# Rows of one tile in every 22nd pair fetched singly by SyncE, and states cleared tile by tile

## The chip, the cores and the metric

The kernel runs on one core of one Trainium2 chip. The metric is the device time of one launch in microseconds (us), as the median of several runs.

## What is computed

The reference is one layer of a graph network (GATv2 with pre-normalization) over 12500 nodes of 128 features and 400000 edges, with a residual and a feed-forward block. The edges come sorted by destination. Cut to what matters here:

```python
h = jnp.maximum(_layernorm(x), 0.0)
x_l = (_ln(h) @ W_l).reshape(n, H, C)          # H = 8 heads, C = 16
x_r = (_ln(h) @ W_r).reshape(n, H, C)
e = (ea @ W_e).reshape(-1, H, C)
m = jax.nn.leaky_relu(x_l[src] + x_r[dst] + e, 0.2)
alpha = jnp.einsum('ehc,hc->eh', m, att)
# softmax of alpha over the edges of each destination, then
out = segment_sum(x_l[src] * a[:, :, None], dst)
h = h + out + bias
return x + h + gelu(_ln(h) @ W1 + b1) @ W2 + b2
```

The costly part is `x_l[src]`: for each of the 400000 edges (and padding) a row of x_l is fetched from DRAM by its source index.

## The kernel before, in words

Nodes lie in 98 tiles of 128. A **preamble** normalizes x, computes x_l for all nodes and writes it to DRAM (`xl_dram`, rows of 136 floats: 128 features and 8 ones, 544 bytes). Its order is written out by hand in rounds `r` (line 784 onwards): at r = 14 the source indices are loaded (`src_sb`, line 797), `as_float` (line 439) and `x_l` (line 595, with its store at 603) run on VectorE (DVE) in their rounds. For 29 chosen pairs of the main loop ("raw" or late pairs) the preamble instead gathers rows of x itself on GpSimd (POOL), and their x_l rows are made later; these pairs need no gather in the main loop.

The **main loop** (`window_edges`) handles 782 pairs. A pair is two units of 256 sorted edges: 512 edges, four tiles of 128 edges. The loop is a software pipeline written out by hand: in round r each stage handles pair r minus its lateness. The stages that matter:

- `gather` (line 972), four rounds ahead: four indirect DMAs on POOL's queue, one per tile, each fetching 128 rows of `xl_dram` into `xs` (line 980). For a late pair, one plain DMA from `late_dram` on SyncE's (SP's) queue instead (line 975). `xs` has twelve buffers.
- `windows` (line 988), three rounds ahead, in every fourth round: four DMAs on SP's queue (`ea`, `dl`, `du`, `zw`, lines 994 to 1010); the address of `zw` comes from a register that SP loads from the SBUF (line 955).
- `place` on DVE (line 1020) turns `dl` into indicator columns in `ea`.
- `combine` on TensorE (PE): four transposes of `xs` (line 1034) and a matmul with `ea` (line 1037) into `z`; then slope, max, scores, minimum, exponent, transposes (lines 1043 to 1088).
- `collect` (line 1097), six rounds late: PE multiplies the turned weights with `xs`.
- `own_heads` (lines 1106 and 1112), seven rounds late, on DVE: the records `rec` of the pair.
- `put` (line 1122), seven rounds late, on SP's queue, last in the round: the records go to the tensor `state` in DRAM, at an address from a register (four addresses are loaded in every fourth round). Records of neighbouring pairs may touch the same nodes, so each store waits for the landing of the one before.

`state` must hold neutral values before the stores come: `clear(g)` (line 743) writes the constant `empty` over seven tiles of nodes, one DMA for each of two states. Group 0 is cleared at the end of the preamble; the other 13 in every eighth round, in the middle of the round.

Until about round 196 SP also loads `ea_s` in every second round for a mean over the edge features (line 1129). Finished groups of four node tiles load their states (`f_state`, line 1173) and go through the feed-forward block in later rounds.

SP issues its DMAs in the order of the program. The program gives them eight semaphores in turn, so that each DMA waits for the landing of the eighth before it. Gathers on POOL have eight semaphores of their own.

Of the kernel before, what the change touches and what calls it, by code (L numbers as in the profile page):

```python
# [13 lines left out]
F32 = mybir.dt.float32  # L14
BF16 = mybir.dt.bfloat16
I32 = mybir.dt.int32
U8 = mybir.dt.uint8
# [5 lines left out]
P = 128  # L23
# [19 lines left out]
OW = 172  # L43
OS = 176
PW = OR * OS
BEFORE = 12
AFTER = 3
WN = P - DE
# [14 lines left out]
BUSY = 5  # L63
LEAD = 2
KEPT = 7
BIG = 2.0**126
CAP = 2.0**120

# [59 lines left out]
def raw_pairs(nt, n_edges):  # L128

    n_pr = -(-n_edges // (UP * U))  # L130
    at = [xr_round(t, nt, n_edges) + XR_STEPS + 1 for t in range(GN, nt, GN)]
    at = at[:-1] + [r + RAW_SHIFT for r in at[:RAW_MORE]]
    return [(r + RAW_STEPS + AHEAD + 1, r) for r in at if r + RAW_STEPS + AHEAD + 2 < n_pr]


def heads_of(nc, pool, out, att_c, fh):
# [8 lines left out]
def tile_gnn(  # L145
# [56 lines left out]
    src_sb = keep.tile([P, NCH * K], I32, name="src_sb")  # L202
    base_sb = keep.tile([1, NU // UP], I32, name="base_sb")
    win_sb = keep.tile([1, NU // QU], I32, name="win_sb")
    flag = keep.tile([1, 1], I32, name="flag")
    quads = [(t, min(GN, NT - t)) for t in range(0, NT, GN)]
    VAR = 6
# [532 lines left out]

    empty = keep.tile([P, H, SH], F32, name="empty")

    def clear(g):
        for st in state:
            nc.sync.dma_start(
                st.rearrange("(t p h) f -> p t (h f)", p=P, h=H)[:, g * GT : (g + 1) * GT, :],
                empty.rearrange("p h f -> p (h f)")[:, None, :].to_broadcast([P, GT, SW]),
            )

    node_stages = (  # L750
        (0, x_stats),
# [16 lines left out]
    with tc.manual_schedule():  # L768
        load_first()
        make_identity(nc, ident)  # L770
        for t in xls:
            nc.vector.memset(t[:, :, P:], 1.0)
        load_weights()
        load_x(0, min(GN, NT))
        load_raw()
        load_x(GN, min(3 * GN, NT - GN))
        for t in range(4 * GN, NT, 14):
            load_x(t, min(14, NT - t))
        load_dst()
        load_consts()  # L780
        nc.vector.memset(empty, 0.0)
        nc.vector.memset(empty[:, :, C + 1 : SH], CAP)
        rows_at = [i * 5 // 4 for i in range(len(raw))]
        for r in range(max(max(len(qs), 9) + LAST + 1, 16 + PARTS, rows_at[-1] + KEPT + 1)):
            if r == 0:
                count_up()
            for d, at in zip(raw, rows_at):
                if r == at:
                    raw_gather(d)
                if r == at + KEPT:  # L790
                    raw_store(d)
            if r == 3:
                weights()
            if r == 9:
                last_of_units()
            if r == 14:
                nc.sync.dma_start(src_sb, src)
# [24 lines left out]
        clear(0)  # L822
    pre.close()

    fast = nc.values_load(flag[0:1, 0:1], min_val=0, max_val=1)
    with tc.If(fast == 1) as cmp:
        window_edges(
            tc, n_edges, ea_t, NT, NE, NUE, ident, wer, weh, negrep, diag, nid, farw, bias_r, b2_r, w1_sb, w2_sb,
            cols, xl_dram, xl_t, xr_dram, xr_t, dc_dram, du_dram, late_dram, state_dram, state, clear, xr_steps, qs, raw_steps, raw, x_t, out_t, h_sb, src_sb, base_sb, win_sb, wid,
        )  # L830
    with cmp.Else():
        any_edges(
# [64 lines left out]

def window_edges(
    tc, n_edges, ea_t, NT, NE, NUE, ident, wer, weh, negrep, diag, nid, farw, bias_r, b2_r, w1_sb, w2_sb,
    cols, xl_dram, xl_t, xr_dram, xr_t, dc_dram, du_dram, late_dram, state_dram, state, clear, xr_steps, qs, raw_steps, raw, x_t, out_t, h_sb, src_sb, base_sb, win_sb, wid,  # L900
):


# [25 lines left out]
    with ExitStack() as es:  # L929
# [34 lines left out]
        def states_at(at):  # L964
# [4 lines left out]
                "u (n f) -> n u f", f=SH * 4  # L969
            )  # L970

        def gather(c):
            xs = rows.tile([P, KP, XW], F32, name="xs")
            if c in of_raw:
                nc.sync.dma_start(xs, late_dram[of_raw[c]["i"]])
                pairs[c]["xs"] = xs
                return
            for t in tiles_of(c):
                for j in t:
                    nc.gpsimd.indirect_dma_start(  # L980
                        out=xs[:, j, :],
                        out_offset=None,
                        in_=xl_dram,
                        in_offset=bass.IndirectOffsetOnAxis(ap=src_sb[:, c * KP + j : c * KP + j + 1], axis=0),
                    )
            pairs[c]["xs"] = xs
# [42 lines left out]
        def combine(c):  # L1029

            d, e = pairs[c], sum(edges_of(c))
            z = ps2.tile([P, EPR], F32, name="z")
            for j in range(e // P):
                nc.tensor.matmul(  # L1034
                    z[:, j * P : (j + 1) * P], d["xs"][:, j, 0:P], ident, start=(j == 0), stop=False, is_transpose=True
                )
            nc.tensor.matmul(z[:, :e], d["zw"], d["ea"][:, :e], start=False, stop=True)  # L1037
            d["z"] = z
# [51 lines left out]
        def collect(c):  # L1090
# [4 lines left out]
            for i, js in enumerate(tiles_of(c)):  # L1095
                for j in js:
                    nc.tensor.matmul(  # L1097
                        d["acc"][:, i, :], d["pt"][:, j * P : (j + 1) * P], d["xs"][:, j, :],
                        start=(j == js[0]), stop=(j == js[-1]),
                    )  # L1100

# [836 lines left out]
```

## Time and profile before

| | |
|---|---|
| median of 3 runs | 3961.41 us (3957.83 to 3962.45) |
| the profiled execution's own time | 3956.45 us |
| its span, first to last instruction | 3954.7 us |
| mean granted TensorE clock | 0.943 |
| DMA moved over the span | 552.09 MB, mean 140 GB/s |

The profile shows one execution. Busy time counts an engine's work, not its waits; for SP the rows named SPq are its issuing of DMAs, its register loads and its moves, in three numbers the least, the median and the longest in ns. In a row of waits stand the total in us, how often, and the longest. In a timeline row stand the start in us, the duration in us, engine, line and operation; in brackets the idle time before it. "issue" is time in which an engine waited for nothing that the profile shows.

### The profile page before, as it was taken

The numbers are of one execution on the slowest core, as the hardware profiler recorded it, in microseconds if no ns is written. First come the engines' busy times: TensorE is split into PE (matmuls) and PEld (weight loads), VectorE is DVE, ScalarE is ACT, GpSimd is POOL, SyncE is SP. The second block draws the span as 40 slices with busy tenths as digits, with TensorE's granted clock in tenths as the row PEclk, the third lists the DMA queues.
The fourth block names the chain that finished last, engine by engine and source line by source line (L and its number), as shares of the span: only waits on it lengthen the run. The fifth ranks groups of instructions, "written<-read, shape, count | busy, mean of one in ns | idle before, by whom it ended". The sixth has DMA issues, their size and how long they took to land. (4 is left out here: it accounts for less than half of the span.)

```text
span 3954.7 us, 58500 instructions
## 1 busy us (share of the span) xinstructions
PE 3447.8 (87%) x18462; PEld 2358.8 (60%) x18463; DVE 2792.9 (71%) x6137; ACT 2168.7 (55%) x4747; POOL 2956.0 (75%) x3138
## 2 busy tenths in 40 slices
PE   4589898989898899999898898998889899889898
PEld 3356565656565666666665665666666566556565
DVE  6577777878776767677767776777767667667665
ACT  7445555655565555555555555555555555455444
POOL 7777777777777777777777777777777777777774
PEclk6799999999999999999999999999999999999999
DMA  8777787777666666666566666556556665655553
GB/s 225 214 183 190 195 201 194 184 176 168 164 128 124 128 122 123 128 123 120 115 122 128 124 123 128 123 119 125 117 124 125 127 122 108 122 119 114 122 118 74
DMA packets 579318, 552.09 MB, mean 140 GB/s; under 512 B 286689, under 2 KB 457282, under 8 KB 578578
## 3 DMA queue, kind: packets, MB, share of 16 engines
q1 hardware_dynamic: 478280, 330.80, 35.9%
q0 software_dynamic: 100000, 217.32, 28.5%
q8 instruction: 150, 2.46, 0.3%
q14 instruction: 168, 1.38, 0.1%
q10 hardware_dynamic: 720, 0.13, 0.0%
HBM read 482.05 MB, written 65.88 MB: 139 GB/s over the span
## 5 line engine op out<-in xcount | busy, mean ns | idle before, releaser
L980 POOL DMA_INDIRECT xs<-xl_dram,src_sb x3009 | 2841.7, 944 | 917.1 <-issue 798.0
L1075 ACT ACTIVATE p<-ab,rec 128x256 f32<-128x256 f32 x1563 | 655.2, 471 | 1025.8 <-DVE rec L1064 1021.3
L1106 DVE TENSOR_TENSOR own<-acc,diag 128x272 f32<-128x272 f32 x782 | 341.4, 437 | 811.5 <-PE acc L1097 809.5
L1097 PE MATMUL acc<-xs,pt 128*128 128x136 f32 x6250 | 891.6, 288 | 0.3 <-DVE own L1106 0.3
L1034 PE MATMUL z<-ident,xs 128*128 128x128 f32 x3125 | 552.9, 283 | 374.0 <-DMA xs<-xl_dram,src_sb 324.9
L1037 PE MATMUL z<-ea,zw 128*128 128x512 f32 x1564 | 852.7, 628 | 26.5 <-DVE ea L1020 11.3
L1034 PEld LDWEIGHTS z<-ident,xs 128*128 128x128 f32 x3125 | 398.4, 143 | 768.4 <-DMA xs<-xl_dram,src_sb 413.6
L1097 PEld LDWEIGHTS acc<-xs,pt 128*128 128x128 f32 x6250 | 820.7, 199 | 0.5 <-DVE own L1106 0.5
L1058 PE MATMUL ab<-m,negrep 128*128 128x512 f32 x1564 | 806.4, 597 | 0.0
L1088 ACT COPY pt<-pt_ps 128x512 f32<-128x512 f32 x782 | 454.9, 582 | 570.9 <-PE pt_ps L1083 568.9
L1053 DVE TENSOR_TENSOR m<-z,zs 128x512 f32<-128x512 f32 x782 | 532.8, 681 | 139.2 <-ACT zs L1048 138.1
L1083 PEld LDWEIGHTS pt_ps<-ident,p 128*128 128x128 f32 x3125 | 415.9, 148 | 360.1 <-issue 286.4
L1020 DVE TENSOR_SCALAR ea<-dl,wid 96x516 f32<-96x516 bf16 x782 | 575.8, 736 | 36.1 <-DMA dl<-dc_dram 36.1
L1064 DVE TENSOR_REDUCE rec<-ab 128x2 f32<-128x512 f32 x781 | 538.0, 689 | 13.1 <-PE ab L1058 12.5
L1083 PE MATMUL pt_ps<-ident,p 128*128 128x128 f32 x3125 | 499.4, 285 | 1.2 <-ACT xr L627 0.9
L1048 ACT ACTIVATE zs<-z 128x512 f32<-128x512 f32 x782 | 472.7, 604 | 41.7 <-DMA xs<-xl_dram,src_sb 34.9
L1112 DVE TENSOR_REDUCE rec<-own 128x34 f32<-128x272 f32 x782 | 340.8, 436 | 26.7
L1043 PE MATMUL ab<-ne,farw 128*128 128x512 bf16 x782 | 313.0, 400 | 28.4 <-ACT p L1075 25.7
L1037 PEld LDWEIGHTS z<-ea,zw 128*128 128x128 f32 x1564 | 256.5, 205 | 30.1 <-DVE ne L1027 10.3
L1058 PEld LDWEIGHTS ab<-m,negrep 128*128 128x128 f32 x1564 | 245.1, 194 | 1.1 <-DMA ea_s<-in_ea_t 0.7
L1043 PEld LDWEIGHTS <-farw 128*128 128x128 bf16 x782 | 79.5, 102 | 221.9 <-issue 110.2
L1075 ACT ACT_TABLE_LOAD x104 | 133.4, 1283 | 1.8
(237 smaller groups left out, 2167.4 us busy)
## 6 DMA issues: line engine op xcount, KB each, us to landing
dl<-dc_dram SPq DMA_DIRECT2D x196, 396.0 KB
ea<-in_ea_t SPq DMA_DIRECT2D x196, 256.0 KB
ea_s<-in_ea_t SPq DMA_DIRECT2D x98, 512.0 KB
xs<-xl_dram,src_sb POOLq DMA_INDIRECT x3009
state<-empty SPq DMA_DIRECT2D x28, 504.0 KB
state<-rec SPq DMA_DIRECT2D x781, 18.0 KB
f_st<-state SPq DMA_DIRECT2D x46, 288.0 KB
du<-du_dram SPq DMA_DIRECT2D x196, 64.0 KB
```

Source lines behind the costliest of these rows:

```text
L980: nc.gpsimd.indirect_dma_start(out=xs[:, j, :], out_offset=None, in_=xl_dram, in_offset=bass.IndirectOffsetOnAxis(ap=src_sb[:, c * KP + j ...
L1020: nc.vector.tensor_scalar(d["ea"][0:WN].rearrange("p (a b) -> p a b", b=OW), d["dl"][0:WN].rearrange("p (a b) -> p a b", b=OS)[:, :, 0:OW] ...
L1034: nc.tensor.matmul(z[:, j * P : (j + 1) * P], d["xs"][:, j, 0:P], ident, start=(j == 0), stop=False, is_transpose=True)
L1037: nc.tensor.matmul(z[:, :e], d["zw"], d["ea"][:, :e], start=False, stop=True)
L1048: nc.scalar.activation(d["zs"][:, :e], d["z"][:, :e], AF.Copy, scale=SLOPE)
L1053: nc.vector.tensor_tensor(d["m"][:, :e], d["z"][:, :e], d["zs"][:, :e], op=OP.max)
L1058: nc.tensor.matmul(d["ab"][:, :e], negrep.rearrange("p n h -> p (n h)"), d["m"][:, :e], start=False, stop=True)
L1064: nc.vector.tensor_reduce(d["rec"][:, :, CX], d["ab"].rearrange("p (u e) -> p u e", e=U), AX.X, OP.min)
L1075: nc.scalar.activation(d["p"][:, us], d["ab"][:, us], AF.Exp, bias=d["rec"][:, i, CX:SH], scale=-1.0)
L1083: nc.tensor.transpose(d["pt_ps"][:, js], d["p"][:, js], ident)
L1088: nc.scalar.copy(d["pt"][:, :e], d["pt_ps"][:, :e])
L1097: nc.tensor.matmul(d["acc"][:, i, :], d["pt"][:, j * P : (j + 1) * P], d["xs"][:, j, :], start=(j == js[0]), stop=(j == js[-1]),)
```

## The change

Two things change.

First, in 35 pairs (31, 53, 75 and so on, every 22nd) the fourth tile isn't gathered by POOL. SP fetches its 128 rows one by one, each with a DMA of 544 bytes at an address from a register, into one of two new tiles `hand0` and `hand1`. The 128 DMAs are spread over 22 rounds, five or six at the start of each round, and end three rounds before `combine` uses the tile. The addresses come from a table `hand_sb` of source indices times the row's size, loaded in the preamble at r = 14 and multiplied on DVE at r = 16; SP loads 26 of them into registers at a time. `combine` and `collect` read the new tile through `row_of`.

Second, `clear` handles one tile of nodes for both states in one DMA. Four tiles are cleared at the end of the preamble, the other 94 one in every fourth round, at the very end of the round, behind `put`.

```diff
+CLEARED = 4
+CLEAR = 4
+HAND_EVERY = 22
+HAND_FIRST = 31
+HAND_LEAD = 2
+HAND_READ = 26
+def hand_pairs(nt, n_edges):
+    late = {c for c, _ in raw_pairs(nt, n_edges)}
+    hands = range(HAND_FIRST, n_edges // (UP * U), HAND_EVERY)
+    assert not late & set(hands)
+    return hands
...
-    def clear(g):
-        for st in state:
-            nc.sync.dma_start(
-                st.rearrange("(t p h) f -> p t (h f)", p=P, h=H)[:, g * GT : (g + 1) * GT, :],
-                empty.rearrange("p h f -> p (h f)")[:, None, :].to_broadcast([P, GT, SW]),
-            )
+    def clear(t):
+        both = state_dram[0 : UP * SR].rearrange("(a n) f -> a n f", a=UP)
+        nc.sync.dma_start(
+            both[:, (BEFORE + t * P) * H : (BEFORE + (t + 1) * P) * H].rearrange("a (p h) f -> p a (h f)", h=H),
+            empty.rearrange("p h f -> p (h f)")[:, None, :].to_broadcast([P, UP, SW]),
+        )
...
             if r == 14:
                 nc.sync.dma_start(src_sb, src)
+                nc.sync.dma_start(
+                    hand_sb,
+                    bass.AP(
+                        tensor=src.tensor, offset=src.offset + (hands[0] + 1) * UP * KU - 1,
+                        ap=[[hands.step * UP * KU, len(hands)], [NCH * K, P]],
+                    ),
+                )
+            if r == 16:
+                nc.vector.tensor_scalar(hand_sb, hand_sb, float(XW * 4), None, op0=OP.mult)
...
-        clear(0)
+        for t in range(CLEARED):
+            clear(t)
...
+        def hand(r):
+            i, k = divmod(r + HAND_LEAD + hands.step - hands[0], hands.step)
+            if not 0 <= i < len(hands):
+                return
+            d = by_hand[hands[i]]
+            if k == 0:
+                d["x"] = once.tile([P, XW], F32, name=f"hand{i % 2}")
+            for e in range(P * k // hands.step, P * (k + 1) // hands.step):
+                if e % HAND_READ == 0:
+                    d["at"] = words(hand_sb[i : i + 1, e : min(e + HAND_READ, P)], (NT * P - 1) * XW * 4)
+                nc.sync.dma_start(
+                    d["x"][e : e + 1, :].bitcast(U8), rows_at(xl_dram, d["at"][e % HAND_READ], 1, XW * 4)
+                )
+        def row_of(c, j):
+            return by_hand[c]["x"] if c in by_hand and j == KP - 1 else pairs[c]["xs"][:, j, :]
...
                 for j in t:
+                    if c in by_hand and j == KP - 1:
+                        continue
                     nc.gpsimd.indirect_dma_start(
...
-        CLEAR = 8
         with tc.manual_schedule():
             for r in range(-AHEAD, max(last_round, groups[-1]["round"] + 18)):
                 in_round(r, early, groups[:-2])
+                hand(r)
...
-                if r > 0 and r % CLEAR == 0 and r // CLEAR < NT // GT:
-                    clear(r // CLEAR)
...
                 for late, f in late_stages:
                     c = r - late
                     if 0 <= c < n_pr:
                         f(c)
+                t, off = divmod(r, CLEAR)
+                if off == 0 and CLEARED <= t + CLEARED < NT and t >= 0:
+                    clear(t + CLEARED)
```

More of the change, by code (lines that the diff above doesn't have):

```diff
@@ L204, in tile_gnn @@
     win_sb = keep.tile([1, NU // QU], I32, name="win_sb")
+    hands = hand_pairs(NT, n_edges)
+    hand_sb = keep.tile([len(hands), P], I32, name="hand_sb")
     flag = keep.tile([1, 1], I32, name="flag")
@@ L828, in tile_gnn @@
             tc, n_edges, ea_t, NT, NE, NUE, ident, wer, weh, negrep, diag, nid, farw, bias_r, b2_r, w1_sb, w2_sb,
-            cols, xl_dram, xl_t, xr_dram, xr_t, dc_dram, du_dram, late_dram, state_dram, state, clear, xr_steps, qs, raw_steps, raw, x_t, out_t, h_sb, src_sb, base_sb, win_sb, wid,
+            cols, xl_dram, xl_t, xr_dram, xr_t, dc_dram, du_dram, late_dram, state_dram, state, clear, xr_steps, qs, raw_steps, raw, x_t, out_t, h_sb, src_sb, base_sb, win_sb, hand_sb, hands, wid,
         )
@@ L899, in window_edges @@
     tc, n_edges, ea_t, NT, NE, NUE, ident, wer, weh, negrep, diag, nid, farw, bias_r, b2_r, w1_sb, w2_sb,
-    cols, xl_dram, xl_t, xr_dram, xr_t, dc_dram, du_dram, late_dram, state_dram, state, clear, xr_steps, qs, raw_steps, raw, x_t, out_t, h_sb, src_sb, base_sb, win_sb, wid,
+    cols, xl_dram, xl_t, xr_dram, xr_t, dc_dram, du_dram, late_dram, state_dram, state, clear, xr_steps, qs, raw_steps, raw, x_t, out_t, h_sb, src_sb, base_sb, win_sb, hand_sb, hands, wid,
 ):
@@ L970, in states_at @@
             )
+        by_hand = {c: {"i": i} for i, c in enumerate(hands)}
+        def hand(r):
[13 more added lines that the diff above has]
+            return by_hand[c]["x"] if c in by_hand and j == KP - 1 else pairs[c]["xs"][:, j, :]
         def gather(c):
@@ L1034, in combine @@
                 nc.tensor.matmul(
-                    z[:, j * P : (j + 1) * P], d["xs"][:, j, 0:P], ident, start=(j == 0), stop=False, is_transpose=True
+                    z[:, j * P : (j + 1) * P], row_of(c, j)[:, 0:P], ident, start=(j == 0), stop=False, is_transpose=True
                 )
@@ L1097, in collect @@
                     nc.tensor.matmul(
-                        d["acc"][:, i, :], d["pt"][:, j * P : (j + 1) * P], d["xs"][:, j, :],
+                        d["acc"][:, i, :], d["pt"][:, j * P : (j + 1) * P], row_of(c, j),
                         start=(j == js[0]), stop=(j == js[-1]),
```

## The prediction

> **What bounds the kernel now.** I read the busy shares first, then the group of the gathers, then the first and the last gather in the timeline, then who waits for them.
>
> ```profile
> PE 3447.8 (87%) x18462; PEld 2358.8 (60%) x18463; DVE 2792.9 (71%) x6137; ACT 2168.7 (55%) x4747; POOL 2956.0 (75%) x3138
> ```
> ```profile
> L980 POOL DMA_INDIRECT xs<-xl_dram,src_sb x3009 | 2841.7, 944 | 917.1 <-issue 798.0
> ```
> ```profile
> 151.60 0.94 POOL L980 DMA_INDIRECT xs<-xl_dram,src_sb  x1 [0.30 <-issue]
> ...
> 3909.17 0.94 POOL L980 DMA_INDIRECT xs<-xl_dram,src_sb  x1 [0.31 <-issue]
> ```
> ```profile
> PE z L1034 <- DMA xs<-xl_dram,src_sb: 324.9, 247, 4.1
> ```
>
> By share PE looks like the bound and POOL looks a quarter idle. The group says otherwise: 2841.7 us busy and 917.1 us idle make 3758.8 us for 3009 gathers, and 0.30 us of "issue" stands ahead of each. From 151.60 to 3909.17 lie 3008 steps of 1.249 us: POOL hardly ever waits for anybody between the first gather and the last. PE meanwhile waits 324.9 us for gathers to land. So POOL's issuing of gathers sets the length of the loop, at 1.249 us each, and each gather taken away is worth that much until something else is late.
>
> **What the change takes away.** 35 pairs (31, 53, ... 779) gather three tiles instead of four: 35 x 1.249 = 43.7 us off the engine that sets the end. No gather is replaced on POOL. PE is the next engine; it must give up 43.7 of its 324.9 us of waiting, so it doesn't become the bound. Its transposes and its collecting matmuls read the new tile instead of xs, same shapes, plus some seven semaphore waits for each such pair, hidden in the same waiting.
>
> **What it adds.** 35 x 128 = 4480 one-row DMAs on SP's queue (about 5.8 in each round, ahead of the round's other work), 175 register loads of up to 26 words, one small table load and one DVE multiply in the preamble, and 98 clears of one tile and both states in place of 28 of seven tiles and one state. All hang on SyncE, so its queue has to be priced. These are its rows: a stretch of it, its operations, its one-row DMAs, its waits, and the landing of stores in the chain that ended last.
>
> ```profile
> 1011.56 0.41 SPq L994 DMA_DIRECT2D ea<-in_ea_t  x1
> 1012.03 0.42 SPq L999 DMA_DIRECT2D dl<-dc_dram  x1
> 1012.50 0.60 SPq L1004 DMA_DIRECT2D du<-du_dram  x1
> 1014.00 0.34 SPq L1010 DMA_DIRECT2D zw<-xr_dram  x1
> 1016.20 0.41 SPq L1122 DMA_DIRECT2D state<-rec  x1
> 1016.66 0.47 SPq L1129 DMA_DIRECT2D ea_s<-in_ea_t  x1
> ```
> ```profile
> L1122 SPq MOVE state<-rec x782: 29/29/38, 183.0 to 3930.3; - x196
> L1122 SPq DMA_DIRECT2D state<-rec x782: 350/395/1278, 192.0 to 3930.4; - x196
> ```
> ```profile
> L955 SPq TENSOR_LOAD <-win_sb x196: 527/748/812, 158.7 to 3896.8; - x196
> L955 SPq TENSOR_LOAD <-base_sb x196: 299/307/331, 182.6 to 3926.9; - x196
> ```
> ```profile
> L745 SPq DMA_DIRECT2D state<-empty x28: 377/488/687, 153.4 to 665.0; - x28
> ```
> ```profile
> L1010 SPq DMA_DIRECT2D zw<-xr_dram x196: 332/343/359, 159.6 to 3897.6; - x196
> ```
> ```profile
> 27.89 0.22 SPq L328 DMA_DIRECT2D dc<-in_dst  x1
> 28.16 0.32 SPq L333 DMA_DIRECT2D dc<-in_dst  x1
> 28.52 0.27 SPq L337 DMA_DIRECT2D dc<-in_dst  x1
> ```
> ```profile
> SPq L1122 <- DMA state<-rec: 1359.2, 547, 8.2
> SPq L1122 <- DVE rec L1112: 739.1, 425, 8.9
> SPq L1122 <- DMA state<-empty: 85.8, 14, 9.3
> ```
> ```profile
> 3926.48 1.65 DMA state<-rec
> ...
> 3928.27 2.02 DMA state<-rec
> ```
>
> SP's work repeats every four rounds. Today: one set of windows, 2.83 us (1011.56 to 1014.34 and the gap behind); four stores at about 0.52 with move, semaphore and gaps, 2.1; one load of four bases, 0.36. While the edge sums are loaded (two rounds of every four, until about round 196) 1.04 more. The late rows and x_r add about 0.25, the finishing groups later about 0.35. That is 6.6 us early and 5.9 us after round 196. The rest of SP's time is waiting, 1359.2 us for a store's landing and 739.1 us for DVE. This waiting is the cover for the new DMAs: they stand between a store and the next one.
>
> Available for four rounds at the new pace: 16 gathers less those that late pairs (29 with no gather, 11 of them in the first 196 rounds) and the new pairs save. Early (784 - 44 - 8) / 196 x 4 x 1.249 = 18.7 us; later about 19.1 us.
>
> Price of a one-row DMA: no row shows one with an address from a register. Bounds: 0.22 us, the shorter of two rows of one descriptor (L328; the other, L337, took 0.27), and 0.395, the store's median, with a register address and 256 pieces. zw, with a register address and 96 rows, takes 0.343; L333, 96 rows and a fixed address, 0.32, so the register costs about 0.02. I take 0.25, between the two one-row rows, plus 0.03 for the move and two gaps of 0.045: 0.37 each. Four rounds hold 23.3 of them, 8.6 us. Register loads: 0.9 per four rounds at 0.75 plus gap, 0.7 us (0.3 by the other row).
>
> The clears: every fourth round until about round 376 one DMA of 0.49 plus gap stands right behind a store of the same tensor and waits for its landing, 1.65 to 2.02 us by the chain: 2.5 us per four rounds. Behind that wait stand the next round's one-row DMAs, its windows and its store. The next store waits for the clear's landing, which the one-row DMAs between them cover. The 85.8 us of waits for the big clears go, but nothing late hung on them, so that is worth nothing.
>
> Sum for SP in four rounds: early 6.6 + 8.6 + 0.7 + 2.5 = 18.4 of 18.7 us; rounds 196 to 376 17.7 of 19.1; then 15.2 of 19.2. It fits, early by a hair. Windows are fetched three rounds ahead, records of stores have eleven buffers, and the one-row tiles are complete three rounds before their use, so SP may lag some 10 us before anyone else waits. I charge 2 us for stretches where a landing is slow.
>
> **Preamble.**
>
> ```profile
> 71.97 0.70 SPq L797 DMA_DIRECT2D src_sb<-in_src  x1
> ...
> 136.65 0.37 SPq L603 DMA_DIRECT2D xl_dram<-xl  x1
> ```
> ```profile
> 43.91 0.61 SPq L266 DMA_DIRECT2D first_sb<-in_dst  x1
> ```
> ```profile
> 77.81 0.42 DVE L439 CAST df<-dc 98x512 f32<-98x512 int32 x1
> ```
>
> The table of 4480 single words is issued right behind src_sb at 72.7; 784 single words took 0.61 us to issue, so 0.6 to 3.5 us here. DVE multiplies it just ahead of the cast that ran at 77.81, so DVE waits for the landing, behind the whole of src_sb. What DVE loses moves the last x_l store from 136.65; the first gather at 151.60 needs that landed (2 us), so 13 us of cover. Bounds: 0 us lost, and some 10 us if DVE stands for more than 20. I take 2.
>
> **Sum.** -43.7 + 2 + 2 = -39.7 us. The profiled execution took 3956.45 us (span 3954.7), giving 3916.7; the median of the runs is 4.96 higher, 3961.41, so **3922**.
>
> [...]
>
> **Rivals.**
> 1. SP becomes the bound in the early loop. For: SP fits with 0.3 us to spare, and landings are slower there. Against: the one-row rows. If each costs 0.34 like zw (0.46 with move and gaps, 10.7 us per four rounds), SP needs 20.5 of 18.7 early and 19.8 of 19.1 until round 376: 49 x 1.8 + 45 x 0.7 = 120 us lost, less 10 of lag: 3922 + 110 = 4032, slower. It cancels the gain at about 0.30 us an issue (19.6 of 18.7, 49 x 0.9 = 44): that price decides.
> 2. The same with the store's price, 0.395 (12.0 us per four rounds): 49 x 3.1 + 45 x 2.0 = 242, so about 4164. The rows of one descriptor speak against it. [...]
> 3. The preamble's wait exceeds its cover: 3922 + 10 = 3932, still faster.
> 4. It doesn't do what it says: the program still issues all gathers. The code skips them, so I leave it out.
>
> **Chances.** Forecast, with small overruns, 0.55; rival 1 in its degrees 0.27; rival 2 0.08; rival 3 0.07; anything else 0.03. Range: the floor is all 43.7 us and 8 us of noise and luck at the ends, 3910; the top is rival 1 at zw's price, 4032, rounded to 4035. Rival 2 and a little more stay out. Faster by over 0.2% (8 us, about what a measurement of this kernel can tell from no change): the forecast, rival 3 and no more, less small overruns, 0.58; within 0.2%, rival 1 near its break-even, 0.08; slower 0.34. The likeliest case alone would be 3912 to 3940.
>
> **What would show it.** Right: 2974 gathers at 1.249 us without gaps, the last one starting near 3867; SP's one-row DMAs at 0.22 to 0.28 us; SP's waits at the store for DVE smaller but still there. Wrong: gaps between POOL's gathers in the first 1900 us, ended by PE; DVE waiting for dl (L1020) or PE for the one-row tile; stores lagging their records by over 10 us; DVE idle for long at the new multiply.

## The result, and the profile after

The changed kernel takes **4393.13 us** (median of 4 runs, 4387.0 to 4399.74) beside 3960.08 us for the kernel before in the same comparison: a ratio of 1.1094, 95% interval 1.1075 to 1.1113. The change costs 433 us where a gain of 39 was forecast, and the time lies far above the top of the range. The profiled execution has a span of 4385.2 us at a mean granted clock of 0.902 (before: 3954.7 us at 0.943).

Line numbers of the changed kernel are some 50 higher than before: the gathers are L1029, the one-row DMAs L1011, all register loads L981, the clears L761, the stores of the states L1171, the window mask L1069. The first lines are the busy shares and the group of the gathers.

```profile
PE 3542.8 (81%) x18462; PEld 2425.4 (55%) x18463; DVE 2794.4 (64%) x6138; ACT 2146.4 (49%) x4747; POOL 2923.4 (67%) x3103
```
```profile
L1029 POOL DMA_INDIRECT xs<-xl_dram,src_sb x2974 | 2808.9, 945 | 1357.7 <-issue 777.1 <-PE acc L1146 496.1 <-DMA xs<-xl_dram,src_sb 33.8
```

The 35 gathers are gone and a gather still costs 0.945 us, so the gain was booked as forecast. But POOL now stands idle 1357.7 us, and 496.1 of these end with a collecting matmul of PE: a buffer for the gathered rows comes free too late. POOL is no longer the bound. PE is busy 95.0 us longer than before for the same 18462 instructions, with the lower clock; how much of the 433 us that adds was not tested. Who is late first is in the waits of all engines (waited for; us in total, times, longest):

```profile
DVE ea L1069 <- DMA dl<-dc_dram: 598.3, 134, 11.3
POOL xs L1029 <- PE acc L1146: 496.1, 159, 12.7
PE z L1086 <- DMA zw<-xr_dram: 265.4, 57, 9.7
```

DVE waits for a window row (dl), PE for another (zw), up to 11 us at a time. Both are fetched by SyncE, three rounds ahead. So SyncE is behind, and its own waits say that it has no air left:

```profile
SPq L761 <- DMA state<-rec: 251.6, 91, 4.8
SPq L1171 <- DMA state<-rec: 120.8, 184, 3.3
SPq L1011 <- DMA dl<-dc_dram: 105.1, 136, 2.1
...
SPq L1171 <- DVE rec L1161: 35.1, 78, 3.9
```

The last row is the one to read. When SyncE waits at a store for DVE's record, it is ahead of the computation. It did so for 739.1 us before and does so for 35.1 us now. What it waits for instead are landings: 251.6 us at the clears, for the store just ahead of them. The one-row DMAs (L1011) wait too, 105.1 us for dl: each DMA waits for the landing of the eighth before it, and that can be one of the windows.

The rows of SyncE's new operations (duration in ns: minimum, median, maximum):

```profile
L1011 SPq DMA_DIRECT2D hand<-xl_dram x4480: 224/228/397, 187.7 to 4325.1; - x195
```
```profile
L981 SPq TENSOR_LOAD <-win_sb x196: 556/805/870, 159.6 to 4327.5; - x196
L981 SPq TENSOR_LOAD <-base_sb x196: 302/562/765, 189.3 to 4353.6; - x196
L981 SPq TENSOR_LOAD <-hand_sb x175: 1619/2132/5929, 185.7 to 4308.6; - x175
```

A one-row DMA takes 0.228 us, inside the forecast 0.22 to 0.28. A register load of 26 words was forecast at 0.75 us and takes 1.6 to 5.9. Summed over its 175 records that is 602 us, 3.44 each, in two heaps: the first, third and fifth load of a tile take 2.16, 1.92 and 1.74 us on average, the second and the fourth 5.68 and 5.70. In SyncE's timeline (start us, us from the first to the last of a stretch of like instructions) such a load is hidden inside a stretch of one-row DMAs:

```profile
1310.48 0.42 SPq L1171 DMA_DIRECT2D state<-rec  x1
1310.99 1.90 SPq L1011 DMA_DIRECT2D hand<-xl_dram  x6
1314.21 0.42 SPq L1171 DMA_DIRECT2D state<-rec  x1
1314.75 7.33 SPq L1011 DMA_DIRECT2D hand<-xl_dram  x4
```

Six DMAs in 1.90 us are 0.32 a step; the four below took 7.33 because a load of 5.58 us stands among them. Both kinds are on the chain of work that ended last, the loads (L981) with 4% of the span and the one-row DMAs (L1011) with 4%:

```profile
PE 38%; DMA 24%; DVE 12%; SPq 11%; issue 5%; ACT 5%; POOL 2%; DVEq 0%; ACTq 0%; POOLq 0%
PE acc L1146 9%; PE z L1086 9%; PE ab L1107 7%; DMA dl<-dc_dram 7%; DMA state<-rec 6%; PE pt_ps L1132 5%; SPq L981 4%; SPq L1011 4%; PE z L1083 3%; DMA zw<-xr_dram 3%; DMA du<-du_dram 3%; PE ab L1092 2%; DVE ea L1069 2%; DVE rec L1113 2%; POOL xs L1029 2%
```

Where the loss falls is seen from the gathers in two stretches (POOL's busy time and its instructions):

```profile
300.00:1000.00 700.00, 417.92 (x443) 0.86 0.61 142
2000.00:3500.00 1500.00, 1054.89 (x1118) 0.93 0.57 117
```

The kernel before has 561 and 1201 gathers there. The first stretch lost 21%, the second 7%. By the starts of the stores, the change lags the kernel before by 245 us at pair 196, by 373 us at pair 376 and by 427 us at the last pair: most is lost early.

### The profile page after: what moved, and what is told of

Same layout as the page of the kernel before. It is cut to its first block, busy times and chain, and to the rows that moved or that the text cites. A ratio compares the mean times of both kernels' runs of the same rounds, so it can differ in the third digit from the quotient of the medians.

```text
span 4385.2 us, 67585 instructions
## 1 busy us (share of the span) xinstructions
PE 3542.8 (81%) x18462; PEld 2425.4 (55%) x18463; DVE 2794.4 (64%) x6138; ACT 2146.4 (49%) x4747; POOL 2923.4 (67%) x3103
## 4 chain that ended last, share of the span: by engine, by line
PE 38%; DMA 24%; DVE 12%; SPq 11%; issue 5%; ACT 5%; POOL 2%; DVEq 0%; ACTq 0%; POOLq 0%
PE acc L1146 9%; PE z L1086 9%; PE ab L1107 7%; DMA dl<-dc_dram 7%; DMA state<-rec 6%; PE pt_ps L1132 5%; SPq L981 4%; SPq L1011 4%; PE z L1083 3%; DMA zw<-xr_dram 3%; DMA du<-du_dram 3%; PE ab L1092 2%; DVE ea L1069 2%; DVE rec L1113 2%; POOL xs L1029 2%
## 5 line engine op out<-in xcount | busy, mean ns | idle before, releaser
L1029 POOL DMA_INDIRECT xs<-xl_dram,src_sb x2974 | 2808.9, 945 | 1357.7 <-issue 777.1
L1086 PE MATMUL z<-ea,zw 128*128 128x512 f32 x1564 | 903.8, 662 | 437.7 <-DMA zw<-xr_dram 265.4
L1069 DVE TENSOR_SCALAR ea<-dl,wid 96x516 f32<-96x516 bf16 x782 | 576.9, 738 | 606.6 <-DMA dl<-dc_dram 598.3
L1146 PE MATMUL acc<-xs,pt 128*128 128x136 f32 x6180 | 907.0, 293 | 21.5 <-DVE own L1155 12.2
L1146 PEld LDWEIGHTS acc<-xs,pt 128*128 128x128 f32 x6180 | 835.9, 204 | 24.4 <-DVE own L1155 12.9
L1107 PE MATMUL ab<-m,negrep 128*128 128x512 f32 x1564 | 816.9, 605 | 0.0
L1083 PEld LDWEIGHTS z<-ident,xs 128*128 128x128 f32 x3090 | 387.4, 145 | 535.0 <-issue 303.2
L1132 PEld LDWEIGHTS pt_ps<-ident,p 128*128 128x128 f32 x3125 | 427.8, 152 | 404.8 <-issue 309.0
L1083 PE MATMUL z<-ident,xs 128*128 128x128 f32 x3090 | 489.7, 280 | 189.6 <-issue 84.1
L1132 PE MATMUL pt_ps<-ident,p 128*128 128x128 f32 x3125 | 516.0, 292 | 20.9 <-ACT pt L1137 15.4
L1184 DVE TENSOR_REDUCE part<-ea_s 128x1 f32<-128x1024 f32 x98 | 119.0, 1214 | 104.1 <-DMA ea_s<-in_ea_t 103.9
```

Of the source, the lines that this page charges most:

```text
L1029: nc.gpsimd.indirect_dma_start(out=xs[:, j, :], out_offset=None, in_=xl_dram, in_offset=bass.IndirectOffsetOnAxis(ap=src_sb[:, c * KP + j ...
L1069: nc.vector.tensor_scalar(d["ea"][0:WN].rearrange("p (a b) -> p a b", b=OW), d["dl"][0:WN].rearrange("p (a b) -> p a b", b=OS)[:, :, 0:OW] ...
L1083: nc.tensor.matmul(z[:, j * P : (j + 1) * P], row_of(c, j)[:, 0:P], ident, start=(j == 0), stop=False, is_transpose=True)
L1107: nc.tensor.matmul(d["ab"][:, :e], negrep.rearrange("p n h -> p (n h)"), d["m"][:, :e], start=False, stop=True)
L1132: nc.tensor.transpose(d["pt_ps"][:, js], d["p"][:, js], ident)
L1146: nc.tensor.matmul(d["acc"][:, i, :], d["pt"][:, j * P : (j + 1) * P], row_of(c, j), start=(j == js[0]), stop=(j == js[-1]),)
```

## The experiments

Two groups of chips have to be kept apart. On one the kernel before took 3961 us, as in the first comparison. On four others it took 4716 to 4765 us, and its trace shows other gaps there (last section). Every run below is given by its ratio to the kernel before on its own chip, with that kernel's time.

**The theories at the start.** A: SyncE is full over the whole loop; its register loads are the largest part of the excess, the clears' wait for the store ahead of them the second. B: the 4480 one-row DMAs alone fill it. C: the clears alone do it.

**The change once more**, unaltered, as a measure for its neighbours:

> The change itself once more, as the measure for its neighbours: the four runs before this one stood against a kernel before of 4716 us in place of 3960, so times go by their ratio to it. 1.109 if this chip behaves as the first one; any other ratio shows what the chip does to the change, and the neighbours are compared with this one.

Measured 5162.53 us beside 4722.09, ratio 1.0931 (1.0907 to 1.0954): 440 us lost on this chip too.

**Clears as before.**

```
-                t, off = divmod(r, CLEAR)
-                if off == 0 and CLEARED <= t + CLEARED < NT and t >= 0:
-                    clear(t + CLEARED)
+                if r > 0 and r % CLEAR == 0 and r // CLEAR < NT // GT:
+                    clear(r // CLEAR)     # CLEAR = 8, seven tiles, ahead of the round's stores
```

> The change, but with the clears as they were: 28 of seven tiles, one state each, in every eighth round, in the middle of the round. Theory A (SyncE is full over the whole loop; its register loads of 26 words, 3.5 us on average where 0.75 was forecast, are the largest part of the excess, the clears' wait for the store ahead of them, 251.6 us by the profile of the change, the second): about 240 us of waiting go over the first 376 rounds and some 40 come with the big clears, so about 4190. Rival B (the 4480 one-row DMAs alone fill SyncE, the wait at a clear only takes the place of waits elsewhere): within 40 us of the change's 4393. Rival C (the clears alone are what made the change slow): about 3925.

Measured 5114.63 beside 4715.9, ratio 1.0844 (1.0813 to 1.0875). Some 40 us by the difference of the ratios, not 200: C falls here. For A's second term the run says little, because the clears wait much less on such a chip. In the traces of two further runs on this chip with the new clears, below, SyncE waits 67.3 us there (one load) and 78.1 us (loads put first), 34 times each, against 251.6 (91 times) on the first chip.

**One register load for all one-row DMAs.**

```
-                if e % HAND_READ == 0:
-                    d["at"] = words(hand_sb[i : i + 1, e : min(e + HAND_READ, P)], ...)
+                if not fixed:
+                    fixed.extend(words(hand_sb[0:1, 0:8], ...))
```

> The change with a single register load of eight words ahead of the first one-row DMA instead of 175 of up to 26 words: all 4480 one-row DMAs are issued as before, but from eight addresses over and over, so the rows of the new tiles are not those of the reference. Theory A: SyncE gives up 175 x 3.47 = 607 us of work; in rounds up to 376 all of the 0.79 us of each round is gained, later only some 0.25 until POOL bounds again, so about 3995 (3960 to 4040). Rival B: the loads cover waits that then appear elsewhere, so no more than 60 us gained, 4330 or above. Rival C: as rival B.

Measured 4890.97 beside 4715.9, ratio 1.0365 (1.034 to 1.0389): 270 us below the change by the ratios. Less than A's 400, far more than B's 60.

**No one-row DMAs and no loads.**

```
-            for e in range(P * k // hands.step, P * (k + 1) // hands.step):
-                ...
+            if k == 0:
+                nc.vector.memset(d["x"], 1.0)
```

> The change without its one-row DMAs and their register loads; the new tiles are filled with ones once each by DVE, so the rows of 35 tiles are left out. The clears stay behind the store. Theory A: SyncE has 12 us of every four rounds to spare, the clears' wait is covered, POOL bounds with 2974 gathers, so 3917 to 3925, with no gaps between the gathers. Rival B: the same. Rival C: 4100 or more, since the waits of the clears stay. If the 43.7 us of 35 gathers were no gain at all, it would be about 3960.

Measured 4676.59 beside 4715.9, ratio 0.9913 (0.9895 to 0.9932): 39 us gained, near the 43.7 forecast, even with the new clears. All of the loss comes with the fetching by hand. That the 39 us are 35 gathers at 1.249 us is not shown by this run: POOL stands idle 1608.9 us in it, and 220.7 of these end with PE's collecting matmul, so on this chip POOL is not the bound throughout.

**Loads put first in the round.** The two heaps of load times suggested a cause: in the trace the long ones stand directly behind a one-row DMA, the short ones behind a store or a clear.

```
+            at = P * k // hands.step
+            if k % 4 == 0:
+                d["e0"] = at
+                d["at"] = words(hand_sb[i : i + 1, at : min(P * (k + 4) // hands.step, P)], ...)
```

> The change with the register loads put first in a round, six of 23 or 24 words for each pair in place of five of 26, so that each stands behind a store or a clear and none behind a one-row DMA. Theory A with the place as the cause of the 5.5 to 5.9 us that two loads of five take: all loads take about 2.0 us, 35 x (17.3 - 6 x 2.0) = 186 us of SyncE go, of which 140 to 180 are gained: 4215 to 4255. If the long loads come from something else than what stands ahead of them, or rival B holds: 4370 to 4400.

Measured 5345.69 beside 4715.9, ratio 1.1352 (1.1317 to 1.1388): slower than the change. The loads behind stores were the long ones this time:

```profile
L980 SPq TENSOR_LOAD <-hand_sb x210: 317/4884/5562, 249.4 to 5275.7; - x105
```

That theory fell. What the long loads of both kernels have in common is their first word: here the six loads of a tile begin at words 0, 23, 46, 69, 93 and 116 and only those at 0 and 116 were short; in the change they begin at 0, 26, 52, 78 and 104, and those at 26 and 78 were long. Short ones begin at a multiple of four. That is theory A1; A2 is the one that failed here, the neighbour ahead.

**28 words in place of 26**, all first words multiples of four, four loads of five still right behind a one-row DMA.

```
-HAND_READ = 26
+HAND_READ = 28
```

> The change with one number other: the register loads take 28 words instead of 26, so they begin at words 0, 28, 56, 84 and 112 of a row, all multiples of four, and still come directly behind a one-row DMA in four cases of five. Theory A1 (a load whose first word is not a multiple of four goes word by word at 0.21 us each, one whose first word is, by fours at 0.28): 7 fours take about 1.95 us and the last 16 words 1.1, 8.9 us for a pair in place of 17.4, 300 us of SyncE less: by ratio 1.04 to 1.06 (some 4120 to 4200 beside 3960). Theory A2 (what stands ahead of a load sets its time, a one-row DMA being the slow neighbour): four of five loads take 5.6 us or more, 24 us for a pair, by ratio 1.14 to 1.18. Rival B (one-row DMAs alone): no change against the control.

Measured 5016.63 beside 4722.09, ratio 1.0623 (1.06 to 1.0645), just above A1's band of 1.04 to 1.06 and 146 us below the change on the same chip, from one digit. The loads:

```profile
L981 SPq TENSOR_LOAD <-hand_sb x175: 13/1812/2184, 248.9 to 4956.2; - x175
```

No load above 2.2 us: A1 holds, A2 falls. A second time, on another chip:

> The change with loads of 28 words instead of 26, nothing else, once more. Beside a before of 3960: 300 us of SyncE less; in the first 376 rounds 0.39 us a round, all of it gained (147 us), later 0.39 of the 0.17 above before's pace, so about 60: ratio 1.109 less 0.05, 1.05 to 1.065. Rival B (the loads only cover waits that come back): 1.09 or above. Beside a before of 4720: 1.062 as it was.

5096.36 beside 4764.52, ratio 1.0688 (1.0668 to 1.0709), 0.6% more than the first time. No run shows this version beside 3960.

**The loads measured by themselves.**

```
+            to = words(hand_sb[1:2, at : at + n], ...)      # one (at, n) in each round, 400 to 519
+            nc.sync.dma_start(used[row : row + 1, :].bitcast(U8), rows_at(xl_dram, to[-1], 1, XW * 4))
```

> Only a measure of the register loads by themselves: the change without its one-row DMAs and their loads (the rows of 35 tiles are ones), and in rounds 400 to 519 one register load and one one-row DMA that uses its last word, in turn 1 word from word 0 and from 1; 4 from 0, 1 and 2; 24 from 0, 1 and 2; 26 from 0 and from 26; and 26 from 0 and from 26 behind four one-row DMAs. A1 (first word a multiple of four or not): 24 from 0 at 1.7 us, 24 from 1 and from 2 at 5.1, 26 from 0 at 2.0, 26 from 26 at 5.6, the same behind one-row DMAs. A2 (what stands ahead): all loads of 26 words at about 2.0 us, but the two behind one-row DMAs at 5.6.

A first form of this run loaded words that no DMA used. Its trace has no register load of `hand_sb` at all, so it shows nothing of them. Here a DMA uses the last word of each load. The rows of six of these loads, each from a short stretch of the trace: 24 words from word 0, from 1 and from 2; 26 from word 26; then, behind four one-row DMAs, 26 from word 0 and 26 from word 26.

```profile
L984 SPq TENSOR_LOAD <-hand_sb x1: 1623/1623/1623, 2492.9 to 2492.9; - x1
...
L984 SPq TENSOR_LOAD <-hand_sb x1: 4949/4949/4949, 2499.0 to 2499.0; - x1
...
L984 SPq TENSOR_LOAD <-hand_sb x1: 5453/5453/5453, 2505.4 to 2505.4; - x1
...
L984 SPq TENSOR_LOAD <-hand_sb x1: 5502/5502/5502, 2517.5 to 2517.5; - x1
...
L984 SPq TENSOR_LOAD <-hand_sb x1: 2157/2157/2157, 2528.1 to 2528.1; - x1
...
L984 SPq TENSOR_LOAD <-hand_sb x1: 4688/4688/4688, 2534.5 to 2534.5; - x1
```

Single rows scatter on this chip (before takes 4759.63 us there), so medians of ten loads of each kind count: 24 words take 1.62, 4.88 and 5.06 us from word 0, 1 and 2; 4 words 0.32, 1.06 and 0.88; 26 words from word 0 take 1.58 and from word 26 5.41, behind one-row DMAs 1.85 and 5.11. As A1 had it. Of these loads, those from a multiple of four took 0.06 to 0.08 us a word, the others 0.20 to 0.27.

**28 words and the old clears together.**

> The change with loads of 28 words, and with the clears as they were (28 of seven tiles, mid-round, every eighth round). Theory A: SyncE gives up 300 us of load time and about 240 us of waiting behind stores, so that only the first 196 rounds are still bound by it, by about 0.2 us a round: 3940 to 3990 beside 3960, a ratio of 0.995 to 1.008. Rival B: 1.09 or above.

Measured 4946.93 beside 4722.09, ratio 1.0495 (1.0463 to 1.0527). Another 70 us, but 5% stay: on this chip the one-row DMAs still cost that much with the shorter loads, and A's band of 0.995 to 1.008, given for a before of 3960, is missed.

**Half as many one-row DMAs, and only late ones.** Both with 28 words and the old clears: every 44th pair (`HAND_FIRST = 53`, `HAND_EVERY = 44`), and every 22nd from pair 229 on (`HAND_FIRST = 229`).

> Loads of 28 words, clears as they were, and every 44th pair from 53 on: 17 pairs, a tile spread over 44 rounds, so 2.9 one-row DMAs a round in place of 5.8. Theory A beside a before of 3960: 21 us gained, 0.993 to 0.998. Where before takes 4720: SyncE has some 1.9 us of waiting in each round to spare by the run without rows, and the one-row DMAs need 1 to 1.7 us, so 0.995 to 1.015; if one-row DMAs cost by their number whatever the spare time, 1.015 to 1.03.

> Loads of 28 words, clears as they were, and the first hand-fetched pair 229 in place of 31: 26 pairs of 35, all of them behind the loads of the edge sums. Theory A beside a before of 3960: SyncE needs about 4.6 us of 4.78 in each of these rounds, POOL bounds, 26 x 1.249 = 32 us gained, ratio 0.990 to 0.996. Where before takes 4720 the one-row DMAs alone cost 0.15 to 0.3 us a round by the pace of the stores of the run with 35 pairs: 1.005 to 1.02.

Measured beside 4759.63: 4782.7, ratio 1.0054 (1.0034 to 1.0074), and 4892.89, ratio 1.0285 (1.0268 to 1.0303). Half of the DMAs in each round cost a half per cent where all of them cost five, so there is no one price for each DMA. That the cost begins when SyncE's spare time is used up fits this, but is not shown by it. Late ones alone cost 0.8% more than the most that was expected. Repeated:

> The version with loads of 28 words, the clears as they were and hands from pair 229 on (26 pairs) once more. Beside a before of 3960: in the run with all one-row DMAs and one load the stores come every 4.74 us from round 200 to 740, where before took 4.84, and SyncE waits 479 us of 1900 there (1.2 us a round); five loads of 1.8 us for 22 rounds take 0.4 of that, so the gain of 26 gathers stays: 26 x 1.249 = 32 us, ratio 0.990 to 0.996. If SyncE's sum isn't the whole story and the loads' blocking counts, as in the run with loads alone: 0.998 to 1.006. Beside a before of 4720 or more: 1.028 as it was.

4887.84 beside 4764.52, ratio 1.0259 (1.024 to 1.0277), nearly the same. No run shows it beside 3960.

**Loads alone, DMAs alone, and two queues.** These three ran where the kernel before takes 3961.3 us. The first keeps the new clears and all 175 loads but one one-row DMA for each; the second keeps all 4480 DMAs with one load and the old clears; the third has the whole work, half of each tile on ScalarE's queue, with loads that begin at multiples of four.

```
                 if e % HAND_READ == 0:
                     d["at"] = words(...)
-                nc.sync.dma_start(...)
+                    nc.sync.dma_start(...)
```

> The change with all 175 register loads of 26 words but only the one one-row DMA that follows each of them: 175 of 4480, the other rows of the 35 tiles are ones. The loads alone thus, 3.5 us each on average as in the change. If what counts is the sum on SyncE (theory A), 0.8 us a round go into the 2 us of waiting that the run without rows has, and the time is that run's ratio, 0.991, up to 1.000. If a load of 5.6 us costs wherever it stands, because a store or a window behind it is late each time, 70 x 3.6 us and more show: 1.03 or above.

> All 4480 one-row DMAs from eight addresses loaded once (the rows of the new tiles are not those of the reference), and the clears as they were: the one-row DMAs alone. The same with the new clears gave 1.0365, without rows 0.9913. Theory A: the clears' waits for the store go, 60 to 100 us as with the loads in place, so 1.015 to 1.025; what is left above 0.991 is the one-row DMAs with their pauses. If the one-row DMAs were harmless by themselves: 0.991 to 0.997.

```
+            for e in range(half * k // hands.step, half * (k + 1) // hands.step):
+                for b, q, of, n in (("s", nc.sync, 0, 16), ("a", nc.scalar, half, 4)):
+                    if e % n == 0:
+                        d[b] = words(hand_sb[i : i + 1, of + e : of + e + n], ...)
+                    q.dma_start(d["x"][of + e : of + e + 1, :].bitcast(U8), rows_at(xl_dram, d[b][e % n], 1, XW * 4))
```

> Clears as they were, and of each tile rows 0 to 63 fetched by SyncE, rows 64 to 127 by ScalarE's queue, each with its own register loads that begin at multiples of four (16 words on SyncE, 4 on ScalarE). All 35 pairs, the rows of the reference. If SyncE's sum decides (theory A), it now has 2240 one-row DMAs like the run with every 44th pair, and ScalarE, busy 46% of the span, takes 2240: the whole gain of 35 gathers shows, 0.990 to 1.000. If ScalarE's work stands in the chain of each pair, 2.9 DMAs of 0.32 us a round and a load delay it by about 1 us a round: 1.02 or above.

Measured 3980.46, ratio 1.0052 (1.0035 to 1.0069); 3990.27, ratio 1.0074 (1.0057 to 1.0091); 3991.81, ratio 1.0069 (1.0052 to 1.0086). The first and the third lie above A's band; the second lies below it, better than thought. The loads with the new clears cost 19 us and the one-row DMAs with the old clears 29; the change, with loads, DMAs and new clears, costs 433. So C falls here too. The parts don't add: these two nearly fit, all together they don't. (The DMA kernel reads the same eight rows over and over.) One-row DMAs with the new clears, and loads and DMAs with the old ones, have no run beside 3960. The gathers by stretch show where even these lose, the loads first, then the DMAs, then the two queues:

```profile
300.00:1000.00 700.00, 500.45 (x531) 0.93 0.72 168
2000.00:3500.00 1500.00, 1134.09 (x1201) 0.96 0.61 124
```
```profile
300.00:1000.00 700.00, 475.55 (x505) 0.90 0.73 169
2000.00:3500.00 1500.00, 1133.76 (x1202) 0.97 0.61 124
```
```profile
300.00:1000.00 700.00, 475.74 (x504) 0.91 0.73 170
2000.00:3500.00 1500.00, 1133.89 (x1201) 0.98 0.61 124
```

Behind 2000 us all of them gather at the pace of the kernel before, with fewer gathers for each pair, so the gain is there: 317, 313 and 315 stores of pairs start in these 1500 us, 310 before the change, and 2974 gathers in place of 3009 would make 313.6. Ahead of 1000 us they fall behind 561. At pair 196 their stores lag by 57, 80 and 87 us, at the last pair by 20, 30 and 37. SyncE's waits from 300 to 1000 us, first before the change, then with the loads alone:

```profile
SPq L1122 <- DMA state<-rec: 269.9, 119, 5.2
SPq L1122 <- DMA state<-empty: 68.7, 11, 9.3
SPq L1122 <- DVE rec L1112: 58.8, 42, 4.3
```
```profile
SPq L1173 <- DMA state<-rec: 202.2, 86, 4.9
SPq L761 <- DMA state<-rec: 114.0, 34, 4.7
...
SPq L1173 <- DVE rec L1115: 2.1, 6, 0.4
```

Already before the change SyncE waited for DVE's records only 58.8 of these 700 us; the rest of its waiting was for landings of the states' own stores, one behind the other. With the loads and the clears it waits 316 us for landings and next to nothing for DVE: it is late itself, though it "waits" almost half of the time.

The two queues didn't help early. In the same stretch SyncE has new waits, for hand-fetched rows to land, and so has ScalarE, which is on the path of each pair (46.3 us here, 220.9 in the whole span). That these waits took the place of the issue that left SyncE is argued, not tested.

```profile
SPq L1013 <- DMA hand<-xl_dram: 37.0, 31, 3.6
SPq L1173 <- DMA hand<-xl_dram: 27.8, 12, 5.3
```
```profile
ACT pt L1139 <- DMA hand<-xl_dram: 46.3, 44, 3.7
```

**Two queues, late only** (`HAND_FIRST = 229` in the kernel above).

> One-row DMAs shared between SyncE and ScalarE, loads that begin at multiples of four, clears as they were, and hands from pair 229 on: 26 pairs. In the run of both queues with all 35 pairs beside a before of 3961, stores came every 4.76 us from round 200 to 740 (before: 4.84) and every 5.11 us from round 30 to 180 (before: 4.67). So without the early rounds, theory A: 26 x 1.249 = 32 us gained, ratio 0.990 to 0.996 beside a before of 3960. Beside a before of 4720 or more, where instructions come late, each queue has 2.9 one-row DMAs a round as in the run with every 44th pair: 0.995 to 1.010, against 1.026 to 1.028 for one queue. If the loss isn't in the early rounds: 1.005 or more beside 3960.

Measured 4730.18 beside 4718.87, ratio 1.0022 (1.0011 to 1.0033), where one queue had 1.026 to 1.029. It has 26 of the 35 pairs. Of all versions that fetch the reference's rows it comes closest to the kernel before, and none beats it. Whether it does beside 3960 is open: by the second stretch above it should, but that is argued and not measured.

## Why the prediction was wrong

- **The gain came out; that it came in the forecast way is shown only in part.** The run without rows gained 39 us of 43.7, on a chip where POOL waits for PE as well, so there the near agreement may be luck. Beside 3961 the runs of loads alone, DMAs alone and two queues show it behind 2000 us: POOL keeps its pace of 1201 gathers in 1500 us and 1% to 2% more pairs pass.
- **The price of a one-row DMA was right**, and it was the wrong thing to fear. 0.25 us plus 0.12 was charged, 0.228 and a step of 0.32 came out. The prediction said of 0.30 us an issue "that price decides"; the issue stayed below it and the gain was lost several times over. Among the 4480 no more than 0.397 was seen.
- **The failed step is "Register loads: 0.9 per four rounds at 0.75 plus gap, 0.7 us (0.3 by the other row)".** The two rows were loads of 1 and 4 words, and were taken for a price that doesn't depend on the number of words, with no bound from above. The loads cost 3.44 us each: 3.1 us per four rounds. That is 2.4 more than charged, where 0.3 were to spare. The runs show about 0.21 us a word for loads of 24 and 26 words that don't begin at a multiple of four (5.68 and 5.70 for 26 words, 4.88 and 5.06 for 24) and about 0.07 for those that do (1.92 and 1.62).
- **The clears were underpriced.** 2.5 us per four rounds were charged. By the row of L761 they wait 2.8 us each (251.6 / 91), and early they took 3.9 us per four rounds, issue and wait. The waits of SyncE in the stretch from 300 to 1000:

```profile
SPq L761 <- DMA state<-rec: 103.8, 29, 4.8
SPq L1011 <- DMA dl<-dc_dram: 14.1, 18, 1.8
SPq L1171 <- DMA state<-rec: 12.6, 24, 2.1
SPq L1011 <- DMA du<-du_dram: 9.7, 18, 1.5
```

  Their removal brought some 40 us, on a chip where they wait 67.3 and 78.1 us in two runs. What it would bring beside 3960 was not measured.
- **A second step failed: "It fits, early by a hair" was a sum of work, set against the whole time of a round.** It had no term for waits other than the clears'. Both of SyncE's waits, for landings and for DVE, were taken as cover over the whole loop. But stores of the same tensor wait for each other's landing, 1359.2 us in all before the change, so a wait for a landing is cover only for work that stands between those two stores; and of the 739.1 us of waits for DVE only 58.8 stand in the stretch from 300 to 1000. That this is why loads alone and DMAs alone lose there fits their waits, but was not tested by itself.
- **In numbers**, early. Between the stores of pairs 30 and 180 lie 892.5 us, so four rounds took 23.8 us, where 18.4 were forecast for SyncE's sum (before the change they took 18.7). Its instructions in the trace, each with the gap ahead of it and without its waits, divide the 23.8 us so:

| per four rounds, pairs 30 to 180 | forecast | measured |
|---|---|---|
| SyncE's other work | 6.6 | 6.6 |
| one-row DMAs | 8.6 | 7.9 |
| their register loads | 0.7 | 3.2 |
| clears, issue and wait | 2.5 | 3.9 |
| all other waits | none (2 us for the whole loop) | 2.2 |

- **Late rounds.** Here 15.2 of 19.2 us were forecast, and four rounds took 20.0 (the stores of pairs 400 and 570 lie 850.2 us apart; before 820.7). The loads are 2.4 more than charged, waits that the sum hadn't add 2.8, other work 0.2, and the one-row DMAs are 0.6 less. The loads alone would still have fitted here (17.6); with the waits it no longer did.
- **Rival 1's outcome came true, not its cause.** SyncE became the bound, with the gaps at POOL ended by PE and the late dl that the prediction named as signs. But the rival was priced by the issue alone, early and up to round 376, with 4032 us at zw's price and 4164 at the store's (rival 2). The issue was cheap; the loads and the landings did it.
- The preamble's two terms were harmless: the first store of a state starts at 193.9 us, before the change at 192.0.

Shown: the price of the loads and what sets it; that SyncE's sum was too small, and by which terms; that without the fetching by hand nothing is lost (beside 4715.9); and that loads with the new clears, or one-row DMAs with the old ones, cost 19 and 29 us where all together cost 433. Open: how many of the 433 us would go with each of loads, clears and DMAs taken away singly where the kernel before takes 3960 us, since those runs stand beside 4716 to 4765.

## What to carry to other kernels

A queue that waits much may still be full. Count as free the time in which it waits for another engine, stretch by stretch (58.8 of 700 us early, before this change); a wait for a landing is free only for work that stands between the two DMAs. Give waits a term of their own in the sum. Price an operation by its size as well as its kind; a row of a load of one word, 0.75 us, is no price for 26, here 3.44 on average. And let a register load begin at a multiple of four words: here 24 words took 1.62 us from word 0 and 4.88 from word 1.

## What the runs showed of the hardware that wasn't expected

The register loads of 24 and 26 words took about 0.07 us a word from a multiple of four and about 0.2 elsewhere (24 words: 1.62 against 4.88 and 5.06 us). The first words that were quick are 0, 28, 52, 56, 84, 104, 112 and 116, the slow ones 1, 2, 23, 26, 46, 69, 78 and 93. What stood ahead on the queue changed the time of loads of 26 words little (from word 0 1.58 us, behind one-row DMAs 1.85; from word 26 5.41 and 5.11), that of short ones more: the load of four bases took 0.31 us behind a store and 0.57 behind a one-row DMA (medians of 159 loads before the change and of 157 after it).

The kernel before took 4716 to 4765 us on four chips. Its trace was taken on one of them:

> The kernel before, for its trace where it takes 4716 to 4722 us. If these runs are only slower in the clock or in the transfers, SyncE's instructions have the same gaps as in the first trace of before and POOL's gathers still follow each other at 1.249 us. If instructions themselves arrive late here, pauses of 0.6 to 0.75 us that no semaphore ends stand between SyncE's and PE's instructions, and POOL waits for PE: over 250 us of gaps between the gathers.

It took 4766.54 us in that run. A gather has the same 0.944 us, but POOL stands idle 1678.2 us (917.1 on the first chip), 211.1 of them until PE is done; on the first chip it waited for hardly anybody (798.0 of the 917.1 are "issue"). "remote" is a wait whose end the profile can't name.

```profile
L980 POOL DMA_INDIRECT xs<-xl_dram,src_sb x3009 | 2841.2, 944 | 1678.2 <-issue 793.8 <-remote 365.2 <-PE acc L1097 211.1
```

In this trace 699 of SyncE's instructions start over 0.3 us behind the one ahead without a semaphore that ends a wait there; on the first chip there are 27. In the change's trace on another of the four chips, six one-row DMAs, which took 1.90 us above, take up to 5.67, and no load stands among them:

```profile
3005.32 5.67 SPq L1011 DMA_DIRECT2D hand<-xl_dram  x6
```

The 3.77 us more would be 0.75 for each of the five steps between the six, an estimate. Such pauses would make each added instruction dearer there: the run with one load has a ratio of 1.0365 there, the like run with the old clears 1.0074 beside 3961. It is argued, not shown. That instructions arrive late is not shown either: the packets of queue q8, which the page lists as "instruction", take no longer there (150 of them, 1.15 us on average against 1.13 on the first chip). Why these chips do it stays open.
